# A four-layer graph network on one core: the turn of the count blocks one block later, the greatest key subtracted by PE, the normed rows added elsewhere

## The chip, the cores and the metric

The kernel runs on one core of a Trainium2 chip, in one launch. The metric is the device time in microseconds of that launch; lower is better. The engines are named PE (TensorE matmul), PEld (TensorE weight load), DVE (VectorE), ACT (ScalarE), POOL (GpSimd) and SP (SyncE, which here issues DMAs).

## The reference, cut to what matters

The input has 3125 nodes with 256 features and 100,000 edges, sorted by destination. Four layers follow each other; each adds a graph part and a mixer to x, and then a feed-forward part:

```python
xn = _layernorm(x, axis=-1)
x = x + _L0_gnn_ref(xn, edge_index, ...) + _L0_mix_ref(xn[None], ...)[0]
x = x + _L0_ffn_ref(_layernorm(x, axis=-1)[None], ...)[0]
...
```

Layer 0's graph part is a normalised sum over edges. It needs, for every pair of blocks of 125 nodes, how many edges lead from each source to each destination, and the number of edges into each destination (the degree). The mixers of layers 0 and 2 are linear attention:

```python
q = jax.nn.softmax(q, axis=-2) * SCALE
k = jax.nn.softmax(k, axis=-1)
context = jnp.einsum('bhdn,bhen->bhde', k, v)
out = jnp.einsum('bhde,bhdn->bhen', context, q)
...
return out + x
```

The softmax of the keys runs over all nodes. Layer 0's mixer gets the normed rows xn, and its result holds them once more (the "+ x" above). Layer 2's graph part gathers rows by source, weighs them and sums them by destination.

## The kernel before, in words

The nodes lie in 25 blocks of 125 rows: `self.x` and `self.xn` are 125 x 25 x 256 in SBUF, and `self.xt` is the transposed normed matrix. `PIECES` are groups of four blocks (the last has one).

The instructions are written through a layer that orders them for each engine when the kernel is built. So the order on an engine is not always the order of the text: an instruction can stand earlier or later among those that it does not depend on. `together` interleaves several generators by their progress, and `issue_after` puts instructions behind a given one on the same engine. Each engine then runs its own list strictly in order.

`prep` loads the edges, finds where each window of destinations begins and norms x. Then `l0_first` runs two generators beside each other.

- `counts` makes the count matrices. Two one-hot operands are built by DVE for every four runs of 128 edges (`lo`, L509, from the source's low part; `ky`, L512, from the source's block and the destination in its window). PE multiplies them into a bank `t` (L514; two banks), a group of windows at a time. ACT evacuates the group to `ct` (L517) and lets the accumulator sum the row (`chk`), which later tells whether a row has more than 255 edges. Each of the 25 destination blocks b has seven such groups, 175 in all. When a block's groups are done it is turned: PE transposes the 25 pieces of 125 x 125 in four portions of 8, 8, 8 and 1 through one bank `y` (L527), and `evac` copies each to `cd`, by turns on DVE (L179) and on ACT (L181). PE then sums columns (L532, into `dp`, from which the degrees come), SP stores `cd` to `cnt_d` (`move`, L172 and L173), DVE adds the identity to the diagonal of `ct` (L535), and every few blocks SP stores `ct` to `ctt_d`.
- `l0_mix_by_pieces` is layer 0's mixer. `context` first computes the greatest key of each column (L821 to L824), turns it into a row `kmrow`, and then for each block computes keys and values (`mm_tok`, L279), subtracts `kmrow` on DVE (L844), takes the exponential on ACT (L845), copies the values (L847) and adds to the context (L836, L837). After that the queries follow by pieces, and DVE adds the normed rows to x (L989) and the mixer's result (L990).

`l0_gnn` comes next: it scales the node rows (L616, L618, overwriting `self.xn`), reloads the counts from `cnt_d` (`cb`) and multiplies (L636). Layer 2's mixer calls the same `context` beside layer 2's graph part, in which POOL gathers rows (L2031), between about 2010 and 2540 us.

Of the kernel before, what the change touches and what calls it, by code (L numbers as in the profile page):

```python
# [2 lines left out]

# [9 lines left out]
F32 = mybir.dt.float32  # L13
# [110 lines left out]
class Net:  # L124
# [146 lines left out]
    def turn(self, src, dst):  # L271
        for i, w in PIECES:
            self.turn_piece(src, dst, i, w)

    def mm_tok(self, ps, xt, b, w):

        k = xt.shape[1]
        for h in range(k):
            self.nc.tensor.matmul(ps, xt[:, h, b * P:(b + 1) * P], w[:, h, :], start=(h == 0), stop=(h == k - 1))  # L279

# [156 lines left out]
    def counts(self, sb, rk, ck, wk, pt, px, py):  # L437
# [14 lines left out]
        nev = sum(-(-len(w) // (512 // (25 * r))) for r, w in WINDOWS)  # L452
        chk = sb.tile([P, nev], F32, name="chk")
# [35 lines left out]
        n = ev = 0  # L489
        full = None  # L490
        for b, (r, ws) in enumerate(WINDOWS):
# [9 lines left out]
            for w0 in range(0, nw, per):  # L501
                m = min(per, nw - w0)
                t = pt.tile([128, 512], F32, name="t")
                for w in range(m):
                    for j in range(ws[w0 + w][2]):
                        if n % 4 == 0:
                            wide = 25 * max(rs[n:n + 4])
                            lo = wk.tile([128, 128, 4], BF, name="lo", bufs=4)
                            nc.vector.tensor_tensor(lo, i4[:, :128], keys[:, 0, None, n:n + 4]  # L509
                                                    .to_broadcast([128, 128, 4]), op=OP.is_equal)  # L510
                            ky = wk.tile([128, 150, 4], BF, name="ky", bufs=4)
                            nc.vector.tensor_tensor(ky[:, :wide], i4[:, :wide], keys[:, 1, None, n:n + 4]  # L512
                                                    .to_broadcast([128, wide, 4]), op=OP.is_equal)
                        nc.tensor.matmul(t[:, w * 25 * r:(w + 1) * 25 * r], lo[:, :, n % 4],  # L514
                                         ky[:, :25 * r, n % 4], start=(j == 0), stop=(j == ws[w0 + w][2] - 1))
                        n += 1
                nc.scalar.activation(  # L517
                    ct[:, :, w0 * r:(w0 + m) * r].rearrange("p h (w r) -> p w h r", r=r),
                    t[:P, :m * 25 * r].rearrange("p (w h r) -> p w h r", w=m, r=r), AF.Identity,
                    accum_out=chk[:, ev:ev + 1])  # L520
                ev += 1
            cd = wk.tile([128, NB, P], BF, name="cd")
            for h0 in range(0, NB, 8):
                m = min(8, NB - h0)
                x = py.tile([128, 8, 128], BF, name="y")
                for h in range(m):
                    nc.tensor.transpose(x[:, h, :P], turned[:, h0 + h, :], self.ident_b[:P, :P])  # L527
                self.evac(cd[:, h0:h0 + m, :], x[:, :m, :P])
            cf = cd.rearrange("p h s -> p (h s)")
            for h in range(NB):  # L530
                m = 128 if h < NB - 1 else P
                nc.tensor.matmul(dp[:m, h:h + 1], cf[:, h * P:h * P + m], one, start=(b == 0 and h == 0),  # L532
                                 stop=(b == NB - 1 and h == NB - 1), skip_group_check=True)
            self.move(nc.sync, self.cnt_d[b], cf[3:])
            nc.vector.tensor_add(ct[:, b, :P], ct[:, b, :P], self.ident_b[:P, :P])  # L535
            if full is not None:
                self.move(nc.sync, *full)
                full = None
            if b + 1 in STORED:
                full = self.ctt_d[:, :, b0 * P:(b + 1) * P], ct4[:, :, 8:8 + (b + 1 - b0) * P]  # L540
            yield (b + 1) / NB
        self.move(nc.sync, *full)
        assert n == NE1 and ev == nev
# [4 lines left out]

        nc.vector.tensor_scalar(chk, chk, float(FEW), None, op0=OP.is_gt)
        nc.vector.tensor_reduce(self.viol[:P, 3:4], chk, axis=AX.X, op=OP.add)  # L550
# [42 lines left out]
    def l0_gnn(self):  # L593

        nc = self.nc
        with ExitStack() as s:
# [3 lines left out]
            w, bias = self.l0_w  # L600
            di = sb.tile([P, NB], F32, name="di")
# [211 lines left out]
    def context(self, sb, wk, w, wo, mem, share):  # L813
# [17 lines left out]
        nc.vector.tensor_copy(mrow, ps[:, :128])  # L831
# [8 lines left out]
        for b in range(NB):  # L840
            ps = self.bank()
            self.mm_tok(ps[:P, :256], self.xt, b, w[:, :, 128:384])
            k = wk.tile([P, 128], F32, name="k")
            nc.vector.tensor_sub(k, ps[:P, :128], mrow[:P])  # L844
            nc.scalar.activation(k, k, AF.Exp)  # L845
# [4 lines left out]
        if mem is not None:  # L850
            mk, mv, _ = mem
            nc.vector.tensor_sub(mk, mk, mrow[:mk.shape[0]])
            nc.scalar.activation(mk, mk, AF.Exp)
            add(mk, mv, False, True)
# [70 lines left out]
    def l0_mix_by_pieces(self, sb, wk):  # L925
# [19 lines left out]
        for i, c in PIECES:  # L945
# [17 lines left out]
            weighed = nc.vector.tensor_mul(q[:, :4 * n], q[:, :4 * n],  # L963
# [24 lines left out]
            with self.tc.issue_after(weighed.ins):  # L988
                nc.vector.tensor_add(v, v, self.xn[:, b0:b0 + n])  # L989
# [3 lines left out]
    def gen_l0_gnn(self):  # L993
        nc = self.nc
        with ExitStack() as s:
# [9 lines left out]
            y = sb.tile([P, NB, D], F32, name="y")  # L1005
            for b in range(NB):
# [1979 lines left out]
```

## Time and profile before

| what | before |
|---|---|
| median of 3 runs (lowest, highest) | 3721.22 us (3718.6, 3730.57) |
| profiled execution: time, span | 3728.88 us, 3727.0 us |
| mean granted clock of TensorE | 0.931 |
| busy: PE, PEld | 3317.4 us (89%), 2299.0 us (62%) |
| busy: DVE, ACT, POOL | 2403.4 us (64%), 1641.6 us (44%), 723.2 us (19%) |
| counting stage with layer 0's mixer | about 75 to 436 us of the span |
| layer 2's gathers | 2009.9 to 2537.0 us |

The page splits the span into 40 slices; the counting stage lies in the first five of them. Where a view gives a line such as L517, it is a line of the kernel before. A busy time is the union of an engine's instructions, so the durations of a group can sum to more than the busy time when they overlap. Each float32 matmul of this kernel shows as two passes, that is, as two records with two weight loads.

### The profile page before, as it was taken

To read this page: it belongs to the slowest core of one execution; us is meant where nothing else is said; L and a number is where in the kernel's file an instruction comes from. 1 tells how busy PE (TensorE), PEld (TensorE's weight loads), DVE (VectorE), ACT (ScalarE), POOL (GpSimd) and SP (SyncE) were. 2 spreads that over 40 slices of the span, in tenths; PEclk is the share of its full clock that TensorE was granted. 3 is DMA by queue.
4 is the path that set the end of the run, shared out by engine and by line. 5 is a ranking of instruction groups with operands and counts; after the bars stand their busy time and mean duration, and the time that the engine had idled before them with its cause. 6 is when DMAs were issued, how large, how long until landed. Compare 5 with 4: busy or idle time off the path is not lost. (4 is left out here: it accounts for less than half of the span.)

```text
span 3727.0 us, 61744 instructions
## 1 busy us (share of the span) xinstructions
PE 3317.4 (89%) x22027; PEld 2299.0 (62%) x22027; DVE 2403.4 (64%) x8119; ACT 1641.6 (44%) x3742; POOL 723.2 (19%) x702
## 2 busy tenths in 40 slices
PE   3887899699988979999998888998999999999978
PEld 2776699578866655555556677876663443444437
DVE  8878634875555673389246777886376666677663
ACT  3467500022235422223235566653337655556563
POOL 2000000144420420000003777771000000100011
PEclk9886799799989978999999999999999999999989
DMA  4234642356541110000004555445003222122135
GB/s 131 65 97 136 166 113 71 103 180 174 174 104 48 37 36 2 16 9 18 9 1 114 141 142 140 138 131 182 1 9 85 68 59 64 52 63 58 30 109 178
DMA packets 215258, 321.85 MB, mean 86 GB/s; under 512 B 51547, under 2 KB 159078, under 8 KB 214940
## 3 DMA queue, kind: packets, MB, share of 16 engines
q1 hardware_dynamic: 166346, 231.14, 21.7%
q0 software_dynamic: 40672, 83.85, 8.4%
q10 hardware_dynamic: 7922, 2.80, 0.3%
q8 instruction: 177, 2.90, 0.3%
q14 instruction: 141, 1.16, 0.1%
HBM read 248.17 MB, written 78.08 MB: 88 GB/s over the span
## 5 line engine op out<-in xcount | busy, mean ns | idle before, releaser
L2448 ACT ACTIVATE xn<-xn,us 125x1000 f32<-125x1000 f32 (+2 forms) x400 | 399.9, 1036 | 145.5 <-DVE z L2453 140.3
L2453 DVE SCALAR_TENSOR_TENSOR z<-xn,us,cs 125x1000 f32<-125x1000 f32 (+2 forms) x400 | 397.3, 1025 | 101.5 <-PE acc L2469 70.1
L2031 POOL DMA_INDIRECT hg<-hx_d,idx x405 | 402.3, 993 | 165.6 <-issue 101.8
L2469 PE MATMUL acc<-z,xr 125*32 125x500 f32 (+1 forms) x2800 | 367.6, 547 | 18.6 <-DVE z L2453 18.2
L1938 ACT ACTIVATE o<-ky,rest_d 128x50 bf16<-128x50 bf16 (+2 forms) x1190 | 303.1, 340 | 167.1 <-DVE ky L1929 147.4
L285 PE MATMUL ps<-xt,w 128*128 128x500 f32 (+1 forms) x672 | 277.7, 561 | 2.5 <-DMA w<-in_L_ffn_W_dram 1.5
L1661 DVE SCALAR_TENSOR_TENSOR x<-ps,lg,x 125x256 f32<-125x256 f32 x200 | 92.5, 478 | 245.3 <-PE ps L279 245.1
L2058 PE MATMUL acc<-hg,to 128*125 128x256 f32 x810 | 218.3, 410 | 12.3 <-DVE to L2054 11.5
L2469 PEld LDWEIGHTS acc<-z,xr 125*32 125x32 f32 x2800 | 100.1, 110 | 205.6 <-issue 116.1
L2469 PE MATMUL acc<-z,ones 125*32 125x500 f32 (+1 forms) x1400 | 223.8, 540 | 0.0
L636 PE MATMUL ps<-y,cb 125*125 125x256 bf16 x1875 | 209.1, 274 | 6.0 <-ACT y L623 2.7
L636 PEld LDWEIGHTS <-cb 125*125 125x125 bf16 x1875 | 206.2, 137 | 6.7 <-issue 5.9
L285 PEld LDWEIGHTS ps<-xt,w 128*128 128x128 f32 x672 | 125.3, 199 | 116.6 <-issue 103.3
L1650 ACT ACTIVATE h<-ps,bnb,bng 128x500 f32<-128x500 f32 (+1 forms) x112 | 80.5, 722 | 252.4 <-PE ps L285 252.4
L279 PE MATMUL ps<-wo,h 128*125 128x256 f32 x800 | 187.8, 386 | 3.5 <-ACT h L1655 2.6
L279 PEld LDWEIGHTS ps<-wo,h 128*125 128x125 f32 x800 | 142.8, 187 | 65.9 <-ACT h L1655 43.5
L285 PE MATMUL ps<-h,w 128*128 128x500 f32 (+1 forms) x448 | 179.3, 542 | 1.4 <-ACT h L1650 1.0
L2058 PEld LDWEIGHTS acc<-hg,to 128*125 128x125 f32 x810 | 151.8, 198 | 46.4 <-DVE to L2054 24.6
L514 PE MATMUL t<-ky,lo 128*128 128x75 bf16 (+4 forms) x1251 | 140.2, 253 | 34.8 <-ACT ct L517 19.7
L517 ACT ACTIVATE ct<-t 125x500 bf16<-125x500 f32 (+4 forms) x175 | 137.0, 831 | 76.3 <-PE t L514 73.9
L285 PE MATMUL pl<-xbt,w 128*128 128x256 f32 x560 | 152.7, 402 | 9.8 <-ACT xbt L1277 9.2
L2708 POOL DMA_DIRECT2D out_dram<-x x7 | 9.5, 1357 | 721.8 <-DVE x L2426 638.9
(696 smaller groups left out, 6910.4 us busy)
## 6 DMA issues: line engine op xcount, KB each, us to landing
w<-in_L_ffn_w_dram SPq DMA_DIRECT2D x70, 512.0 KB
cs<-ctt_d SPq DMA_DIRECT2D x100, 218.8 KB
lb<-low_d SPq DMA_DIRECT2D x76, 256.0 KB
w<-in_L_ffn_w_dram SPq DMA_DIRECT2D x18, 1024.0 KB
cnt_d<-cd SPq DMA_DIRECT2D x25, 683.6 KB
cb<-cnt_d SPq DMA_DIRECT2D x25, 683.6 KB
ctt_d<-ct SPq DMA_DIRECT2D x5, 2734.4 KB
cs<-ctt_d SPq DMA_DIRECT2D x50, 164.1 KB
```

The lines of the kernel that those rows point to most:

```text
L279: self.nc.tensor.matmul(ps, xt[:, h, b * P:(b + 1) * P], w[:, h, :], start=(h == 0), stop=(h == k - 1))
L285: self.nc.tensor.matmul(ps, w[:, h, :], xt[:, h, i:i + n], start=(h == 0), stop=(h == k - 1))
L514: nc.tensor.matmul(t[:, w * 25 * r:(w + 1) * 25 * r], lo[:, :, n % 4], ky[:, :25 * r, n % 4], start=(j == 0), stop=(j == ws[w0 + w][2] - 1))
L517: nc.scalar.activation(ct[:, :, w0 * r:(w0 + m) * r].rearrange("p h (w r) -> p w h r", r=r), t[:P, :m * 25 * r].rearrange("p (w h r) -> p ...
L636: nc.tensor.matmul(ps[:P, :D], cf[k][:, h * P:(h + 1) * P], y3[:, b0 + k, j, :], start=(k == 0 and j == 0), stop=(k == m - 1 and j == 2))
L1661: nc.vector.scalar_tensor_tensor(self.x[:, b, :], ps[:P, :D], g[:, b, e:e + 1], self.x[:, b, :], op0=OP.mult, op1=OP.add)
L1938: nc.scalar.activation(o1[:, k], ky[:, :, i], AF.Copy, scale=rest[:, k, n + i:n + i + 1])
L2031: nc.gpsimd.indirect_dma_start(out=hg[:, j, :], out_offset=None, in_=hx, in_offset=bass.IndirectOffsetOnAxis(ap=idx[:, c0 + j - CF:c0 + j ...
L2058: nc.tensor.matmul(acc, to, hg[:, j, :D], start=(c == first[kind]), stop=(c == last[kind]))
L2448: nc.scalar.activation(t[:, :n], (tail if one else rows)[:P, h, :n], AF.Relu, bias=us[:, 2, b, h:h + 1], scale=us[:, 0, b, h:h + 1])
L2453: made.append(nc.vector.scalar_tensor_tensor(zs[h], t[:, :n], us[:, 1, b, h:h + 1], c, op0=OP.add, op1=OP.mult).ins)
L2469: mm = nc.tensor.matmul(out[q:q + 32, :w], left, zs[h0 + j][:, k * w:k * w + w], start=(b == 0), stop=(b == NB - 1), tile_position=(0, q))
```

## The change

It has four parts. The evacuation of a window group no longer accumulates; whether there are too many edges is tested on the degrees instead (`many`). The turn of a block, its column sums, its stores and its diagonal are kept as functions in a list `late` and are called one by one behind the evacuations of the next block; all copies of a turned portion are on ACT. In `context` the row `kmrow` holds the negative maximum, and a matmul with one contracted row, written between the two halves of `mm_tok`, adds it to the keys in PSUM; the exponential reads PSUM. The addition of the normed rows leaves the mixer's pieces and is written at the start of `l0_gnn`.

```diff
-    def mm_tok(self, ps, xt, b, w):
+    def mm_tok(self, ps, xt, b, w, first=None):
         k = xt.shape[1]
         for h in range(k):
             self.nc.tensor.matmul(ps, xt[:, h, b * P:(b + 1) * P], w[:, h, :], start=(h == 0), stop=(h == k - 1))
+            if h == 0 and first is not None:
+                part, row = first
+                self.nc.tensor.matmul(part, self.ones[:1, :P], row[:1], start=False, stop=False, skip_group_check=True)
...
+        late = []
+        def turn(cd, turned, h0):
+            m = min(8, NB - h0)
+            x = py.tile([128, 8, 128], BF, name="y")
+            for h in range(m):
+                nc.tensor.transpose(x[:, h, :P], turned[:, h0 + h, :], self.ident_b[:P, :P])
+            nc.scalar.copy(cd[:, h0:h0 + m, :], x[:, :m, :P])
+        def close(b, cd, ct, done):
+            nonlocal full
+            cf = cd.rearrange("p h s -> p (h s)")
+            for h in range(NB):
...
+            self.move(nc.sync, self.cnt_d[b], cf[3:])
+            nc.vector.tensor_add(ct[:, b, :P], ct[:, b, :P], self.ident_b[:P, :P])
+            if full is not None:
+                self.move(nc.sync, *full)
+            full = done
...
                 nc.scalar.activation(
                     ct[:, :, w0 * r:(w0 + m) * r].rearrange("p h (w r) -> p w h r", r=r),
-                    t[:P, :m * 25 * r].rearrange("p (w h r) -> p w h r", w=m, r=r), AF.Identity,
-                    accum_out=chk[:, ev:ev + 1])
-                ev += 1
+                    t[:P, :m * 25 * r].rearrange("p (w h r) -> p w h r", w=m, r=r), AF.Identity)
+                if late:
+                    late.pop(0)()
+            while late:
+                late.pop(0)()
             cd = wk.tile([128, NB, P], BF, name="cd")
-            for h0 in range(0, NB, 8):
-                m = min(8, NB - h0)
-                x = py.tile([128, 8, 128], BF, name="y")
-                for h in range(m):
-                    nc.tensor.transpose(x[:, h, :P], turned[:, h0 + h, :], self.ident_b[:P, :P])
-                self.evac(cd[:, h0:h0 + m, :], x[:, :m, :P])
...
+            late += [partial(turn, cd, turned, h0) for h0 in range(0, NB, 8)]
+            done = (self.ctt_d[:, :, b0 * P:(b + 1) * P], ct4[:, :, 8:8 + (b + 1 - b0) * P]) if b + 1 in STORED else None
+            late.append(partial(close, b, cd, ct, done))
             yield (b + 1) / NB
+        for f in late:
+            f()
         self.move(nc.sync, *full)
...
-        nc.vector.tensor_scalar(chk, chk, float(FEW), None, op0=OP.is_gt)
-        nc.vector.tensor_reduce(self.viol[:P, 3:4], chk, axis=AX.X, op=OP.add)
+        many = sb.tile([P, NB], F32, name="many")
+        nc.vector.tensor_scalar(many, dp[:P, :NB], float(FEW), None, op0=OP.is_gt)
+        nc.vector.tensor_reduce(self.viol[:P, 3:4], many, axis=AX.X, op=OP.add)
...
@@ l0_gnn
+            for i, c in PIECES:
+                v = self.x[:, i // P:(i + c) // P]
+                nc.vector.tensor_add(v, v, self.xn[:, i // P:(i + c) // P])
...
@@ context
-        nc.vector.tensor_copy(mrow, ps[:, :128])
+        nc.vector.tensor_scalar(mrow, ps[:, :128], -1.0, None, op0=OP.mult)
...
-            self.mm_tok(ps[:P, :256], self.xt, b, w[:, :, 128:384])
+            self.mm_tok(ps[:P, :256], self.xt, b, w[:, :, 128:384], first=(ps[:P, :128], mrow))
             k = wk.tile([P, 128], F32, name="k")
-            nc.vector.tensor_sub(k, ps[:P, :128], mrow[:P])
-            nc.scalar.activation(k, k, AF.Exp)
+            nc.scalar.activation(k, ps[:P, :128], AF.Exp)
...
@@ l0_mix_by_pieces
-            with self.tc.issue_after(weighed.ins):
-                nc.vector.tensor_add(v, v, self.xn[:, b0:b0 + n])
             nc.vector.tensor_add(v, v, t[:, :n])
```

The general path, which does not run on this input, gets the same addition of the normed rows at its own graph part.

More of the change, by code (lines that the diff above doesn't have):

```diff
@@ L2 @@
 from contextlib import ExitStack
+from functools import partial
 import numpy as np
@@ L451, in counts @@
         keys = sb.tile([128, 2, NT1 * 128], BF, name="keys")
-        nev = sum(-(-len(w) // (512 // (25 * r))) for r, w in WINDOWS)
-        chk = sb.tile([P, nev], F32, name="chk")
         TB = 2
@@ L488, in counts @@
         dp = self.bank()
-        n = ev = 0
+        n = 0
         full = None
+        late = []
[9 more added lines that the diff above has]
+            for h in range(NB):
+                m = 128 if h < NB - 1 else P
+                nc.tensor.matmul(dp[:m, h:h + 1], cf[:, h * P:h * P + m], one, start=(b == 0 and h == 0),
+                                 stop=(b == NB - 1 and h == NB - 1), skip_group_check=True)
+            self.move(nc.sync, self.cnt_d[b], cf[3:])
[3 more added lines that the diff above has]
+            full = done
         for b, (r, ws) in enumerate(WINDOWS):
@@ L518, in counts @@
                     ct[:, :, w0 * r:(w0 + m) * r].rearrange("p h (w r) -> p w h r", r=r),
-                    t[:P, :m * 25 * r].rearrange("p (w h r) -> p w h r", w=m, r=r), AF.Identity,
-                    accum_out=chk[:, ev:ev + 1])
-                ev += 1
-            cd = wk.tile([128, NB, P], BF, name="cd")
-            for h0 in range(0, NB, 8):
-                m = min(8, NB - h0)
-                x = py.tile([128, 8, 128], BF, name="y")
-                for h in range(m):
-                    nc.tensor.transpose(x[:, h, :P], turned[:, h0 + h, :], self.ident_b[:P, :P])
-                self.evac(cd[:, h0:h0 + m, :], x[:, :m, :P])
[L529 to L540, printed above, removed]
+                    t[:P, :m * 25 * r].rearrange("p (w h r) -> p w h r", w=m, r=r), AF.Identity)
[3 more added lines that the diff above has]
+                late.pop(0)()
+            cd = wk.tile([128, NB, P], BF, name="cd")
+            late += [partial(turn, cd, turned, h0) for h0 in range(0, NB, 8)]
+            done = (self.ctt_d[:, :, b0 * P:(b + 1) * P], ct4[:, :, 8:8 + (b + 1 - b0) * P]) if b + 1 in STORED else None
+            late.append(partial(close, b, cd, ct, done))
             yield (b + 1) / NB
+        for f in late:
+            f()
         self.move(nc.sync, *full)
-        assert n == NE1 and ev == nev
+        assert n == NE1
         few = sb.tile([P, NB], F32, name="few")
@@ L851, in context @@
             mk, mv, _ = mem
-            nc.vector.tensor_sub(mk, mk, mrow[:mk.shape[0]])
+            nc.vector.tensor_add(mk, mk, mrow[:mk.shape[0]])
             nc.scalar.activation(mk, mk, AF.Exp)
@@ L962, in l0_mix_by_pieces @@
             nc.vector.reciprocal(qm[:, :4 * n], qm[:, :4 * n])
-            weighed = nc.vector.tensor_mul(q[:, :4 * n], q[:, :4 * n],
+            nc.vector.tensor_mul(q[:, :4 * n], q[:, :4 * n],
                                            qm[:, :4 * n, None].to_broadcast([P, 4 * n, 32]))
@@ L1005, in gen_l0_gnn @@
             y = sb.tile([P, NB, D], F32, name="y")
+            nc.vector.tensor_add(self.x, self.x, self.xn)
             for b in range(NB):
```

## The prediction

> **What bounds the kernel now.** I read the page first. PE is busy for 89% of the span, DVE for 64%, ACT for 44%, so the whole does not say which engine counts, and I went to the two places that the change touches. The first is the counting of edges beside layer 0's mixer (75 to 436 us of the span), the second layer 2's graph part (2010 to 2540 us). The busy times by stretch of the first, one line for each stretch (length, then PE, PEld, DVE, ACT, POOL busy, granted clock, DMA share, GB/s):
>
> ```profile
> 75.00:110.00 35.00, 24.71 (x254) 20.80 (x255) 33.89 (x130) 6.50 (x17) 0.00 (x0) 1.00 0.01 1
> 110.00:150.00 40.00, 36.41 (x310) 26.55 (x309) 33.32 (x107) 14.31 (x31) 0.00 (x0) 0.76 0.13 41
> 150.00:240.00 90.00, 80.67 (x816) 70.39 (x814) 62.48 (x205) 54.30 (x144) 0.21 (x1) 0.84 0.42 119
> 240.00:340.00 100.00, 81.60 (x865) 69.45 (x861) 83.21 (x237) 71.17 (x176) 0.43 (x2) 0.76 0.47 131
> 340.00:436.00 96.00, 75.85 (x697) 63.27 (x694) 73.76 (x191) 64.74 (x168) 0.42 (x2) 0.66 0.47 122
> ```
>
> Up to 110 us DVE is full (33.89 of 35). From 110 to 240 us PE is nearly full (117.1 of 130), DVE has 95.8 and ACT 68.6. From 240 to 436 us ("late" below) nobody is: PE 157.5, DVE 157.0, ACT 135.9 of 196 us, so there the engines wait for each other. Next I read what PE waited for in the late stretch (microseconds, times, longest):
>
> ```profile
> PE t L514 <- ACT ct L517: 14.2, 43, 0.6
> PE y L527 <- DVE cd L179: 8.5, 14, 1.2
> PE y L527 <- ACT cd L181: 7.5, 12, 1.1
> PE t L514 <- DVE ky L512: 2.0, 2, 1.7
> PE y L527 <- ACT ct L517: 1.8, 3, 0.8
> PE ps L532 <- ACT cd L181: 1.1, 5, 0.4
> ```
>
> PE turns a finished block of counts in four portions through one bank (y), and each portion waits until DVE or ACT has copied the one before: 8.5 + 7.5 + 1.1 = 17.1 us. From 110 to 240 us the same three rows have only 0.4 + 1.3 + 0.6 = 2.3 us, since there the mixer's matmuls fill the gaps. The durations I need, as groups of instructions from 75 to 440 us (busy us, mean ns of one | idle before):
>
> ```profile
> L517 ACT ACTIVATION_READ_ACCUMULATOR ct<-t 125x1 f32 x175 | 36.6, 209 | 0.0
> L179 DVE COPY cd<-y 128x1000 bf16<-128x1000 bf16 x50 | 34.0, 681 | 20.6 <-PE y L527 20.3
> L181 ACT COPY cd<-y 128x1000 bf16<-128x1000 bf16 x25 | 24.7, 989 | 36.4 <-PE y L527 36.2
> L836 PE MATMUL ps<-k,v 125*128 125x128 f32 x50 | 13.7, 365 | 0.0
> L989 DVE TENSOR_TENSOR x<-x,xn 125x1024 f32<-125x1024 f32 x6 | 7.3, 1218 | 0.0
> L844 DVE TENSOR_TENSOR k<-ps,kmrow 125x128 f32<-125x128 f32 x25 | 6.8, 287 | 16.7 <-PE ps L279 15.5 <-ACT cd L181 0.7 <-ACT ct L517 0.4
> L980 ACT ACT_TABLE_LOAD x6 | 7.7, 1283 | 0.1
> ```
>
> **Part 1: the turn of a block moves behind the next block's windows.** In the compiled order of the changed kernel the four turns and the column sums of block b stand between the seven window groups of block b+1, with window matmuls in between that need neither y nor cd. So a copy of 0.99 us has a group of PE work over it. I let the cd waits go: -17.1 late, -2.3 before that. The first turn of a block no longer waits for that block's last evacuation, the rows "y <- ct": 1.8 us late, 1.2 us from 110 to 240 us, so -3.0. What is late next is the evacuation ct, so it needs its own sum.
>
> **Part 2: ACT takes all copies, and the accumulators go.** DVE loses 50 copies, 34.0 us; ACT gains 50 x 0.989 = 49.5 us. ACT loses 175 accumulator reads. By the group that is 36.6 us, but the reads lie half over the evacuation they follow: at 427.60 us an evacuation of 0.77 us starts, its read runs from 428.19 to 428.38, and the next starts at 428.40, a step of 0.80. So a read costs between about 0.03 (0.80 - 0.77) and 0.21 us; I take 0.1, nearer to the step, 17.5 us in the stage. The compiled order has two more activation table loads in the mixer's pieces, 2 x 1.283 = 2.6 us. ACT gains 49.5 + 2.6 - 17.5 = 34.6 us in the stage and about 31.6 (32 copies of 16 blocks) + 2.6 - 11 (112 reads) = 23 us late, so 159 of 196 us: it becomes the fullest engine. In the late stretch ACT sat 31.1 us waiting for the transposes alone ("ACT cd <- PE y"), and these waits go with the new order, so the 23 us fit into time that is idle now. What stands behind a copy in ACT's queue is the next evacuation ct, for which PE waits with two banks. I set the copies ahead of evacuations against the shorter evacuations: 52 waits of PE for ct in the whole stage, some 0.1 us shorter each, -5, and +5 for the copies: 0. The ends are -5 (all hidden) and +45 (nearly every moved copy holds PE once); I stay near zero because ACT has 196 - 135.9 = 60 us free there. Half of the added table loads on the path: +1. The last block's turn has nothing after it: two copies on ACT instead of DVE, 2 x (0.989 - 0.681), +0.6. DVE's relief takes half of PE's waits for ky after 110 us (3.1 us), -1.5.
>
> One rule speaks against this part. The Trainium skill, page "ScalarE: Activation LUTs", section "Rules for kernel authors", sends plain element work to VectorE, which it calls up to about three times faster per element in bf16. The trace's copy out of PSUM has a ratio of 989 to 681 ns, 1.45. By the page's factor an estimate for the copy on DVE would be 0.33 us, the exchange would cost 50 x 0.66 = 33 us more ACT than DVE time instead of 50 x 0.31 = 15.4, and the last flush would lose 1.3 instead of 0.6 us.
>
> **Part 3: the greatest key by PE.** Per layer 25 subtractions leave DVE (25 x 0.287 = 7.2 us) and 25 matmuls with one contracted row come to PE, inside mm_tok between its two halves, with a weight load of their own. The nearest rows are float32 matmuls with 128 moving columns: 25 of them take 13.7 us in 50 passes (L836, with 4 contracted rows its passes are no shorter: 270 to 372 ns). From the start of one to the next matmul it was 0.28 us at full clock (210.65 to 210.93) and 0.53 us at half (224.09 to 224.62). At the stretch's clock of 0.84, a third of the time at half, that is 0.36 us: 25 x 0.36 = +9.0, between 7.0 and 13.7. It lies between 149 and 255 us, where PE is the fullest engine, so all of it is on the path. Below nothing is possible only through DVE: ACT's k waited 8.0 us for that subtraction, but PE waited for neither, so I give it no gain. In layer 2 the same 25 matmuls fall into a stretch that the gather queue sets. Two of its stretches by busy time, and then what POOL waited for from 2080 to 2400 us:
>
> ```profile
> 2150.00:2200.00 50.00, 41.28 (x411) 34.52 (x412) 36.65 (x161) 30.18 (x122) 38.12 (x40) 0.93 0.55 146
> 2200.00:2250.00 50.00, 47.35 (x522) 40.22 (x520) 42.12 (x163) 32.43 (x123) 38.42 (x39) 0.97 0.51 136
> ```
>
> ```profile
> POOL hg L2031 <- issue: 63.1, 207, 0.3
> ```
>
> POOL does 39 or 40 gathers in every 50 us with 0.30 us of issue between them, 1.25 us each, whatever PE does. PE has 3 to 9 us free in each 50 us, against 25 x 0.36 / 6 = 1.5 us that come in; this is the cover. Without it the layer would lose 9 us. I take +1 (0 to 9).
>
> **Part 4: the normed rows.** The seven additions (6 x 1.22 + 0.42 = 7.7 us of DVE) are written at the graph part's head, where 7.7 us would stand before the first scaling. But the compiled order has them in the counting stage, each directly or almost directly behind the addition of the mixer's piece: the same work a few instructions later, cost 0. Were they at the head, up to 7.7 us would be added. The queue of SP keeps its order except that one small store moves two places, and the last block's counts still go out before the reloads, so the 14 us between the last store's issue (436.5) and the first reload (450.8) stay.
>
> **Sum.** -17.1 - 2.3 - 3.0 + 0 + 1 + 0.6 - 1.5 + 9.0 + 1 + 0 = -12.3 us. The profiled execution took 3728.9 us (span 3727.0), 7.7 us above the median of 3721.2; 3728.9 - 12.3 = 3716.6 there, and 3709 us on the median.
>
> **The rivals.**
> Nothing is gained: the fullest engine stays 80% full, as now (157 of 196). With ACT at 159 the late stretch is 198 us, the cd waits come back as ct waits, while the early part has its 9.0 less 2.3 and 1.2: +7 us, 3728 us at the far end, about 3718 if half of the cd waits go. For it speaks that PE waits for ct oftener (43 times) than for cd (31), and that the compiled order leaves some late blocks with 23 to 27 window matmuls in one run and the turns in another; against it ACT's 31.1 us of waiting for turns.
> Slower: the copies in ACT's queue hold the evacuations, and PE stops with both banks t full. Each of the 50 moved copies that does so costs 0.99 us; 12.3 / 0.99 = 12 of them beyond my zero eat the gain, and with 25 it is +12 us, 3734; with all, +37 us, 3758. For it: ACT runs evacuations back to back at 425 to 430 us with PE waiting. It decides once ACT is over nine tenths full late.
> Much faster: the denser order keeps the clock up. If late PE ran at the 0.84 of 150 to 240 us, its 81.6 and 75.85 us would be 73.8 and 59.6, 24 us less: 3709 - 24 = 3685. Against it: the clock fell to 0.5 around 130 to 150 us with PE over eight tenths busy, so density alone does not hold it. The Trainium skill, page "TensorE: Matmul & The Clock Gate", Part 1, ties the low clock to an idle window of about 3.4 us. [...]
>
> **How the numbers follow.** Forecast (gain 5 to 20 us) 0.45, no gain 0.24, slower 0.19, much faster 0.12. 0.3% of the time, 11 us, is about what a measurement of this kernel can tell from no change. Three quarters of the forecast case and the fast one lie beyond it: faster 0.46; the rest of the forecast case and most of the no-gain case: same 0.33; slower 0.21. The range goes from the fast case, 3683, to the slower one with about 24 copies, 3733; the worst of the slow case and a little of the fast one lie outside.
>
> **What would show it.** Late: "PE y <- cd" nearly gone, ACT about 159 us busy and DVE about 135 (157 less 32 x 0.681); the counting ends some 12 us earlier than 436 us; gathers at 39 or 40 per 50 us. From 149 to 255 us 50 more PE passes of 0.27 us or more. Wrong if "PE t <- ACT ct" grows past 30 us, if ACT is nine tenths full, if the clock moves by 0.1, or if the time changes after the graph part's head.

## The result, and the profile after

The changed kernel takes 3735.7 us (median; 3730.8 to 3745.3), the kernel before 3728.2 us (median of as many runs beside it; 3718.6 to 3744.6). The ratio is 1.0019, 95% interval [1.0011, 1.0028]: about 7 us slower, where 12 us faster was forecast. (The forecast counted from 3721.2 us, the median of three runs of the kernel before; over twenty runs that median is 3728.2, so 7 of the 27 us between the forecast 3709 and 3735.7 us lie in the starting point.) The profiled execution took 3737.6 us (span 3735.7), against 3728.9 (span 3727.0).

The stretches of the counting part again, with the columns of the table of before:

```profile
75.00:110.00 35.00, 25.36 (x233) 19.99 (x234) 33.05 (x127) 5.04 (x9) 0.00 (x0) 1.00 0.00 1
110.00:150.00 40.00, 36.34 (x352) 28.06 (x351) 34.10 (x114) 23.21 (x28) 0.00 (x0) 0.83 0.13 41
150.00:240.00 90.00, 87.65 (x911) 74.53 (x910) 53.69 (x181) 65.79 (x119) 0.21 (x1) 0.92 0.43 120
240.00:340.00 100.00, 81.23 (x869) 72.48 (x869) 80.06 (x232) 86.91 (x145) 0.42 (x2) 0.76 0.48 132
340.00:436.00 96.00, 65.17 (x608) 53.63 (x606) 51.49 (x135) 69.37 (x114) 0.42 (x2) 0.64 0.47 121
```

Up to 240 us the change does what it should: PE is busier (149.4 us in 75 to 240 us against 141.8), the granted clock is higher (0.92 for 0.84 in the third row), and the mixer's first product (here and below: of the queries with the context) comes at 259.6 instead of 271.1 us. The late stretch gives it back: PE 146.4 of 196 us where it had 157.5, DVE 131.6 where it had 157.0, ACT 156.3. The last one-hot operand is built at 420.7 instead of 427.0 us, but the last block's store goes out at 437.2 instead of 436.0. What PE waited for from 240 to 436 us (microseconds, times, longest):

```profile
PE t L538 <- ACT ct L541: 18.8, 35, 3.2
PE y L499 <- ACT cd L500: 18.6, 23, 3.4
PE ps L507 <- ACT cd L500: 3.6, 7, 1.1
PE t L538 <- DVE ky L536: 3.2, 3, 2.6
PE y L499 <- ACT ct L541: 2.6, 6, 1.0
```

The waits of the turns for their copies ("y <- cd", "ps <- cd") were 17.1 us. They are 22.2 us now, all of them for ACT, and the longest is 3.4 us instead of 1.2. What lies in such a wait is seen in ACT's own timeline (start, duration, operation; in brackets the idle time before it):

```profile
391.73 0.74 ACT L541 ACTIVATE ct<-t 125x500 bf16<-125x500 f32 x1
392.50 1.28 ACT L995 ACT_TABLE_LOAD   x1
393.79 0.20 ACT L995 ACTIVATE ss<-ss 125x4 f32<-125x4 f32 x1
394.01 1.28 ACT L974 ACT_TABLE_LOAD   x1
395.31 0.31 ACT L974 ACTIVATE q<-q 125x128 f32<-125x128 f32 x1
395.52 0.97 ACT L500 COPY cd<-y 128x1000 bf16<-128x1000 bf16 x1
397.58 0.99 ACT L500 COPY cd<-y 128x1000 bf16<-128x1000 bf16 x1 [1.09 <-PE y L499]
```

and in PE's, where one line answers to it:

```profile
396.55 1.00 PE L499 MATMUL y<-ident_b,ct 125*128 125x125 bf16 x8 [3.39 <-ACT cd L500]
```

The turn ahead of it was done at 391.7 us, but its copy stands in ACT's list behind an evacuation and the mixer's square root and exponential with a table load each. Until 396.5 us nobody may write bank y, and PE stops with everything behind that turn. Then a portion takes 2.07 us each: PE writes y (1.0 us), ACT copies it (0.99), and each idles while the other works (1.09).

Not all waits are of this kind. In 18 of the 30 behind the 22.2 us, 11.9 us together, ACT began the copy within 0.1 us of the turn's end, and PE had less other work than the copy takes before the next turn or column sum. So it is at the stage's end (a line of ACT, then one of PE):

```profile
433.10 0.99 ACT L500 COPY cd<-y 128x1000 bf16<-128x1000 bf16 x1 [1.09 <-PE y L499]
434.14 1.00 PE L499 MATMUL y<-ident_b,ct 125*128 125x125 bf16 x8 [0.92 <-ACT cd L500]
```

In the other 12 waits, 10.3 us, ACT began the copy 0.5 to 10 us after the turn's end.

The groups the prediction spoke of, from 75 to 440 us:

```profile
L541 ACT ACTIVATE ct<-t 125x500 bf16<-125x500 f32 x96 | 78.7, 860 | 27.2 <-PE t L538 25.5 <-PE y L499 1.0
L500 ACT COPY cd<-y 128x1000 bf16<-128x1000 bf16 x75 | 75.4, 1006 | 40.8 <-PE y L499 38.4 <-issue 1.2 <-PE t L538 0.7
L283 PE MATMUL ps<-kmrow,ones 1*125 1x128 f32 x50 | 12.6, 333 | 0.0
L616 DVE TENSOR_TENSOR x<-x,xn 125x1024 f32<-125x1024 f32 x6 | 7.3, 1210 | 0.0
```

ACT still waits 38.4 us for turns in the whole stage for these 75 copies (36.2 us before for 25 of them; DVE had 20.3 for the other 50). From 240 to 436 us it is 29.8 us (24.7 for the long copies, 5.1 for the short), where the prediction took 31.1 us of such waits as idle time that would become free.

The second place is layer 2. From the first gather to the last sum over gathered rows it took 541.4 us before and 548.9 us after, and layer 2's gathering began at nearly the same moment (2009.9 and 2010.6 us), since some 3 us by which layer 0 was behind (the first reload of the counts came at 453.9 instead of 450.8 us) were made up on the way. POOL's gathers (shortest, median and longest in ns, then first and last start):

```profile
L2045 POOL DMA_INDIRECT hg<-hx_d,idx x405: 942/949/2162, 2010.6 to 2543.0; - x135
```

Before, the last started at 2537.0 us.

### The profile page after: what moved, and what is told of

Its sections match the earlier page's. It is cut to its first block, busy times and chain, and to the rows that moved or that the text cites. A ratio compares the mean times of both kernels' runs of the same rounds, so it can differ in the third digit from the quotient of the medians.

```text
span 3735.7 us, 61750 instructions
## 1 busy us (share of the span) xinstructions
PE 3321.8 (89%) x22127; PEld 2302.7 (62%) x22127; DVE 2364.4 (63%) x8019; ACT 1681.6 (45%) x3619; POOL 725.2 (19%) x702
## 3 DMA queue, kind: packets, MB, share of 16 engines
q1 hardware_dynamic: 166346, 231.14, 22.2%
## 5 line engine op out<-in xcount | busy, mean ns | idle before, releaser
L2483 PE MATMUL acc<-z,xr 125*32 125x500 f32 (+1 forms) x2800 | 367.1, 548 | 19.2 <-DVE z L2467 18.8
L533 DVE TENSOR_TENSOR lo<-i,keys 128x512 bf16<-128x512 bf16 x313 | 131.1, 419 | 62.7 <-PE t L538 61.7
L538 PE MATMUL t<-ky,lo 128*128 128x75 bf16 (+4 forms) x1251 | 137.1, 254 | 34.7 <-ACT ct L541 20.2
L541 ACT ACTIVATE ct<-t 125x500 bf16<-125x500 f32 (+3 forms) x175 | 137.1, 836 | 37.4 <-PE t L538 35.5
```

Source lines behind the costliest of these rows:

```text
L541: nc.scalar.activation(ct[:, :, w0 * r:(w0 + m) * r].rearrange("p h (w r) -> p w h r", r=r), t[:P, :m * 25 * r].rearrange("p (w h r) -> p ...
L2483: mm = nc.tensor.matmul(out[q:q + 32, :w], left, zs[h0 + j][:, k * w:k * w + w], start=(b == 0), stop=(b == NB - 1), tile_position=(0, q))
```

## The experiments

The runs were made on several chips. On those of e5 to e8 and e13 to e18 the kernel before takes 3951 to 3960 us instead of some 3728, so ratios are to the kernel before on the same chip, and moments of the counting part are compared with e16, the changed kernel itself there. On that kind of chip the changed kernel itself has one run, e16: 3971.2 us where the kernel before has 3959.9, 1.0028. "Counting ends" is the issue of the last store of a block's counts. Moments and stretches are read from one profiled execution of each kernel.

**The parts alone (e1 to e3).** e1 has only the counting part of the change; e2 only the key by PE; e3 is the changed kernel with layer 2's key subtracted by DVE again:

```diff
+            if mem is None:                       # layer 2
+                self.mm_tok(ps[:P, :256], self.xt, b, w[:, :, 128:384])
+                nc.vector.tensor_add(k, ps[:P, :128], mrow[:P])
+                nc.scalar.activation(k, k, AF.Exp)
...
```

> Only the counting part of the change (turns one block later, all copies on ACT, no accumulators); the greatest key and the normed rows as before. Theory A (in the counting stage DVE stops at the diagonal addition and so gives the gain back; the 7.6 us lost after 2005 us belong to the key matmuls in layer 2): the counting stage ends near 436 us, layer 2 costs nothing, the time is that of before within 4 us. Rival B (the key matmuls in the counting stage ate a gain of the turns): the counting stage ends near 427 us and the time is about 9 to 12 us below before.

> Only the greatest key by PE, in both layers; the rest as before. Theory A: layer 2 loses about 7 us, the counting stage 0 to 5 us: 7 to 12 us above before. Rival C (the loss in layer 2 is a matter of the order that the counting part brings, or noise of one profile): 0 to 2 us above before, or 9 us in the counting stage and nothing in layer 2.

> The changed kernel, but in layer 2 DVE adds the negative greatest key and no key matmul is run there. Theory A: layer 2's last product of gathered rows ends some 7 us earlier than in the changed kernel for the same start of the gathers, and the time is 7 us below the changed kernel, near that of before. Rival C: no difference from the changed kernel within 3 us.

Ratios 1.0001 [0.9992, 1.0010], 0.9996 [0.9988, 1.0005] and 1.0010 [1.0001, 1.0020]. Counting ended at 433.4, 431.5 and 440.7 us. Neither part alone is slower than before; both together are. The price of the key in layer 0 depends on what stands beside it: without deferral the mixer's first product comes earlier with it (271.1 to 265.4 us), with deferral later (252.6 to 259.6). Layer 2's stretch is 545.3, 545.2 and 541.9 us. So e3's stretch is the 7 us shorter that was expected, but its median is only 3.4 us below the changed kernel's, with intervals that overlap.

**The diagonal, the copying engine, the normed rows (e4 to e6).** e4 adds the identity to a block's diagonal one block later, e5 gives half of the copies back to DVE, e6 puts the normed rows back into the mixer's pieces.

```diff
-            nc.vector.tensor_add(ct[:, b, :P], ct[:, b, :P], self.ident_b[:P, :P])
+            while diag:                                   # e4, in close
+                c = diag.pop(0)
+                nc.vector.tensor_add(c, c, self.ident_b[:P, :P])
+            diag.append(ct[:, b, :P])
...
-            nc.scalar.copy(cd[:, h0:h0 + m, :], x[:, :m, :P])
+            self.evac(cd[:, h0:h0 + m, :], x[:, :m, :P])  # e5, in turn
...
+            with self.tc.issue_after(weighed.ins):        # e6, in the mixer's pieces
+                nc.vector.tensor_add(v, v, self.xn[:, b0:b0 + n])
```

> The changed kernel, with the diagonal addition of block b put behind the turns of block b+1 instead of its own. Theory A: DVE no longer waits for the turns there (20.8 us from 340 to 437 us and 5.8 us from 240 to 340 us), window matmuls follow sooner, and the counting stage ends about 10 us earlier, at some 427 us; the time is about 3726. Rival D (ACT, with all copies, binds the late stretch): the waits of DVE move to the one-hot builders and the stage ends within 3 us of 437.

> The changed kernel with the copies of turned portions by turns on DVE and ACT, as before. Theory F (the turns that are left behind the last one-hot operands, 15.7 us in the changed kernel against 8.3 before, take back what the counting won): the chain of that tail has three copies of 0.99 us of which one or two become 0.68, so 1 to 3 us below the changed kernel. Rival D (ACT, which has all copies, binds the late stretch): 8 us or more below it.

> The changed kernel with the normed rows added in the mixer's pieces, as before. The prediction's term (0, since the compiled order had the additions in the counting stage anyway): within 3 us of the changed kernel. Rival E (the new place costs something in the counting stage): 4 to 8 us below the changed kernel.

Ratios 1.0023 [1.0012, 1.0035], 1.0053 [1.0035, 1.0071] and 1.0050 [1.0032, 1.0068]; counting ended at 445.5, 438.6 and 440.4 us (e16: 439.2). None of the three is the cause. That ACT takes all copies is not what costs: with DVE back in, the waits of turns and sums for copies from 240 to 430 us are still 16.2 us (20.2 in the changed kernel). The Trainium skill, page "ScalarE: Activation LUTs", section "Rules for kernel authors", sends plain element work to VectorE; here half of the copies on VectorE moved the end by 0.6 us, less than two profiles of one kernel differ (437.2 and 439.2 us).

**A second bank (e7), and the key in layer 0 alone (e8).** e7 is the changed kernel with the turned portions alternating between bank y and the bank x of the window keys; e8 is the kernel before with the key by PE in layer 0 only.

```diff
-            x = py.tile([128, 8, 128], BF, name="y")
+            x = (px.tile([128, 8, 128], BF, name="x") if h0 // 8 % 2 else py.tile([128, 8, 128], BF, name="y"))
```

> The changed kernel with two PSUM banks by turns for the turned portions (the second is the bank that the keys used at the start), so that PE can turn a portion while ACT copies the one before. Theory F: the tail behind the last one-hot operands falls from 15.7 to about 10 us and the waits of PE for a copy (15.5 us from 340 to 437 us) go: 5 to 10 us below the changed kernel. Rival D: ACT's copies keep the pace, 0 to 2 us below.

> The kernel before with the greatest key by PE in layer 0 only. From the profiles (the key part alone ended the counting 4.5 us earlier and lengthened layer 2 by about 4.6 us): layer 2 as before, the counting some 4 us shorter, so about 4 us below before, at 3725. Rival: the shorter counting was noise of one profile, and the time is that of before.

Ratios 1.0037 [1.0019, 1.0055] and 1.0001 [0.9981, 1.0020]. With two banks counting ended at 430.3 us, 9 us before e16. PE's waits for copies from 240 to 436 us in e7:

```profile
PE ps L507 <- ACT cd L500: 8.7, 15, 1.5
PE y L499 <- ACT cd L500: 6.1, 8, 1.9
PE x L499 <- ACT cd L500: 0.8, 2, 0.5
```

The portions wait 6.9 us instead of 17.7 (e16), but the column sums 8.7 instead of 3.6, so 15.6 us in all instead of 21.3. e8's counting ended at 430.4 us, as its expectation had it, but the whole doesn't show the 4 us: its interval holds both that gain and none.

**Twice the key, the last blocks in place, and two candidates (e9 to e12).** e9 runs the one-row matmul twice with half of the maximum. e10 turns the last two blocks behind their own window groups. e11 is the changed kernel with two banks and with layer 2's key on DVE; e12 is the kernel before with two banks and layer 0's key by PE, so without deferral.

```diff
-                self.nc.tensor.matmul(part, self.ones[:1, :P], row[:1], start=False, stop=False, skip_group_check=True)
+                for _ in range(2):                # e9, and mrow times -0.5
+                    self.nc.tensor.matmul(part, self.ones[:1, :P], row[:1], start=False, stop=False, skip_group_check=True)
...
             late.append(partial(close, b, cd, ct, done))
+            while late and b >= NB - 2:           # e10
+                late.pop(0)()
```

> The changed kernel with the one-row matmul done twice for each block, each with half of the greatest key, so 50 instead of 25 of them in each of the two layers. Theory (the one-row matmuls are paid on PE, in layer 0 where PE is full and in layer 2 too, where the forecast gave them only 1 us): layer 0's stage ends 3 to 9 us later and the stretch from the first gather to the last sum of layer 2 grows by another 4 to 5 us, some 8 to 13 us over the changed kernel, ratio to before about 1.004 to 1.006. Rival (the loss in layer 2 is one of order, not of PE time): layer 2's stretch stays at about 547 us and the whole within 4 us of the changed kernel, ratio about 1.002.

> The changed kernel, but the last two of the 25 blocks are turned behind their own window groups instead of one block later, so that nothing but one block's turn is left behind the last one-hot operand. Theory (the loss of the counting part is the tail of turns that nothing fills): the time from the last ky to the last store falls from 16.5 us to 9 to 11 us, and the counting stage ends at about 430 to 432 us instead of 437; the whole gains 5 to 7 us over the changed kernel, ratio to before about 1.000. Rival (the tail only shows work that was late already): the last ky comes as much later as the tail gets shorter, the end stays at 436 to 438 and the ratio at 1.002.

> The changed kernel with two banks for the turned portions and with the greatest key subtracted by DVE again in layer 2. Theory (the two places that lose are the chain through one bank at the end and the one-row matmuls of layer 2): counting ends 6 to 9 us earlier than in the changed kernel, layer 2's stretch is 4 to 5 us shorter, 10 to 13 us in all, so 3 to 6 us below before, ratio 0.9985 to 0.999. Rival (the two do not add up, since the clock takes back what the order gives): the same as before or slower, ratio 1.000 to 1.001.

> The kernel before with the key subtracted by PE in layer 0 alone, and with two banks for the turned portions, whose copies DVE and ACT share as before; neither the deferred turns nor the change of the normed rows. Theory (the waits of turns for copies, 17 us late, can be had by a second bank, without deferring anything): counting ends 3 to 8 us before 436 us and the whole is 3 to 8 us below before, ratio 0.998 to 0.999. Rival (the bank taken from the window keys and the clock give it back): no difference, ratio 1.000.

e9: 1.0065 [1.0051, 1.0080]. Counting ended 19 us later than in the changed kernel (456.4), 0.77 us for each of 25 more matmuls, twice what the prediction took. Of this only 0.42 us are PE's own time, from the first pass of such a matmul to the start of the next one (mean of 50). Layer 2's stretch was 548.0 us, no longer than with one (548.9): there the rival was right.
e10: 1.0020 [1.0010, 1.0031]. The time from the last one-hot to the last store fell from 16.5 to 10.3 us, but the last one-hot came 6.5 us later (427.2), and counting ended at 437.5. I had taken the long tail for the cause; it is not. The rival held: it only shows work that is late already.
e11: 0.9990 [0.9981, 0.9999], counting ended at 427.9. e12: 0.9981 [0.9970, 0.9992], counting ended at 422.4, median 3720.0 against 3727.6 us. The version without deferral has the lower median of the two, by 3.5 us, though the intervals overlap.

**Is it the order? (e13 to e16).** In the changed kernel's compiled order the turns of late blocks stand in pairs or threes with 20 to 30 window matmuls in one run before them, not one by one as the text has them. e13 pins PE to the text, e14 does so with e11's edits, e15 is the kernel before with the second bank and nothing else, e16 the changed kernel again.

```diff
+            with self.tc.issue_after(put[0].ins):         # in turn: behind the last window matmul
                 for h in range(m):
-                    nc.tensor.transpose(x[:, h, :P], turned[:, h0 + h, :], self.ident_b[:P, :P])
+                    put[0] = nc.tensor.transpose(x[:, h, :P], turned[:, h0 + h, :], self.ident_b[:P, :P])
...
+                        with self.tc.issue_after(put[0].ins) if put[0] is not None else ExitStack():
                             mm = nc.tensor.matmul(t[:, w * 25 * r:(w + 1) * 25 * r], lo[:, :, n % 4],
```

> The changed kernel with its PE order pinned to the text: every turned portion issues behind its window group and ahead of the next one, so that 4 to 10 window matmuls stand between two portions all through the stage. Theory (the deferral brought nothing because the compiled order puts the turns together again): the waits of the turns for copies after 240 us fall from 19.5 us to below 8, the counting stage ends at 425 to 431 us instead of 437, the whole 6 to 12 us below the changed kernel, ratio to before 0.999 to 1.001. Rival (one bank and ACT's queue of evacuations and mixer work set the pace in any order): the waits move to the window matmuls (t for ct above 25 us after 240 us), the stage ends at 435 us or later, ratio 1.001 to 1.004.

> As e13, but with two banks for the turned portions and with the greatest key subtracted by DVE in layer 2. Theory: what is left of the waits goes, counting ends at 420 to 427 us, and the whole is 5 to 12 us below before, ratio 0.997 to 0.9985. Rival (ACT's queue is the bound): no better than the two banks without the pinned order, 428 us and ratio 0.999.

> The kernel before with two banks for the turned portions and nothing else changed. Theory (the 17 us of waits of turns for copies belong to the single bank): these waits fall to about 6 us after 240 us, counting ends 4 to 9 us earlier than 436 us, ratio 0.998 to 0.999. Rival (the gain of the earlier run with two banks came from the key by PE in layer 0): the waits fall but the stage ends within 3 us of 436, ratio 1.000.

> The changed kernel once more, for a second profile. Theory: the same waits in the late stretch (turns for copies 19 to 20 us, windows for evacuations 18 to 19), the counting ending between 435 and 440 us, and layer 2's stretch from first gather to last sum between 546 and 550 us. If these move by more than 4 us, differences of that size between single profiles say nothing.

e13: 1.0041 [1.0021, 1.0061], counting ended at 438.4. PE's waits from 240 to 436 us in e13:

```profile
PE y L501 <- ACT cd L502: 32.7, 16, 5.3
PE ps L509 <- ACT cd L502: 6.7, 9, 1.3
PE t L541 <- ACT ct L545: 6.7, 18, 0.5
PE y L501 <- ACT ct L545: 4.9, 12, 1.0
```

So the compiled order alone was not at fault: the stage ends where the rival put it, though not by the rival's waits. The window groups now wait less for evacuations (6.7 us), but fewer and longer waits stand at the turns; 29.3 of the 39.4 us are behind a copy that ACT began more than 0.2 us after the turn's end. At 342.1 us PE was done with the windows behind a turn and then stood 5.08 us before the next turn, while ACT worked through evacuations, two table loads and the mixer's activations ahead of the copy (lines of ACT, then one of PE):

```profile
342.24 0.60 ACT L545 ACTIVATE ct<-t 125x500 bf16<-125x500 f32 x1
342.86 1.28 ACT L999 ACT_TABLE_LOAD   x1
344.15 0.20 ACT L999 ACTIVATE ss<-ss 125x4 f32<-125x4 f32 x1
344.37 1.28 ACT L978 ACT_TABLE_LOAD   x1
345.67 0.63 ACT L978 ACTIVATE q<-q 125x512 f32<-125x512 f32 x1
346.20 0.97 ACT L502 COPY cd<-y 128x1000 bf16<-128x1000 bf16 x1
347.23 1.00 PE L501 MATMUL y<-ident_b,ct 125*128 125x125 bf16 x8 [5.08 <-ACT cd L502]
```

e15: 0.9979 [0.9962, 0.9997], counting ended at 424.2 us. The same view of e15:

```profile
PE t L514 <- ACT ct L517: 16.4, 49, 0.7
PE t L514 <- DVE ky L512: 7.2, 8, 2.8
PE x L527 <- ACT cd L181: 2.2, 2, 1.1
PE ps L532 <- DVE cd L179: 1.9, 5, 0.4
PE y L527 <- ACT ct L517: 1.7, 3, 0.7
...
PE y L527 <- DVE cd L179: 1.3, 2, 1.0
```

The waits for copies are 5.9 us in all by PE's list (0.5 us of it in a row not shown), and they did not come back as waits for evacuations (16.4 for 14.2); only the waits for the one-hot ky rose, by 5 us. One bank more does what the deferral was to do. Not all of the 12 us reach the graph part: the first reload of the counts came 20 us after the last store (at 444.5 us, in e12 at 442.6), in the other kernels 15 to 17, so it is 6 us earlier than before (450.8). e14: 0.9979 [0.9961, 0.9997], counting ended at 430.2, no earlier than in e11, and with 21.1 us of waits for copies, as many as in e16. So the end of the stage doesn't go by these waits alone. e16: waits of 17.7, 3.6 and 19.3 us in the first three kinds, counting ended at 439.2, so single profiles of one kernel agree within some 2 us here. Layer 2's stretch was 783.1 us on that chip, so its expected moment holds only for the others.

**The two that were left (e17, e18).** All kernels with deferred turns have the mixer's last product at 395 to 420 us and then 23 us or more of counting alone; those without have it 1 to 13 us ahead of the end. e17 reports the counting's progress a block later, so that the mixer is written a block later. e18 keeps both PE's matmul and DVE's addition in layer 2, half of the maximum each.

```diff
-            yield (b + 1) / NB
+            yield b / NB                          # e17
...
-            nc.scalar.activation(k, ps[:P, :128], AF.Exp)
+            if mem is None:                       # e18; mrow times -0.5 in layer 2
+                nc.vector.tensor_add(k, ps[:P, :128], mrow[:P])
+                nc.scalar.activation(k, k, AF.Exp)
```

> The changed kernel, but the counting reports its progress one block later, so that the mixer's work is interleaved one block later. Theory (the late stretch loses since the deferral brings the mixer's end ahead and leaves counting alone): the mixer's last product moves from 401 us to 415 us or later, the counting ends at 427 to 433 us instead of 437, the whole 4 to 10 us below the changed kernel, ratio to before 0.999 to 1.001. Rival (the one bank holds the counting whatever lies beside it): the mixer ends later, the counting still at 436 us or later, ratio 1.001 to 1.003.

> The changed kernel, but in layer 2 PE adds half of the negative maximum and DVE the other half, so that the one-row matmul and DVE's addition are both there. Theory (what costs in layer 2 is PE's matmul between the halves): the stretch from the first gather to the last sum stays at 546 to 550 us, or at 4 us above that of a kernel without the matmul on the same chip, ratio as the changed kernel's, 1.002. Rival (what costs is the other order that the missing addition brings): the stretch goes back to 541 to 545 us, ratio 1.000 to 1.001.

e17: 1.0052 [1.0031, 1.0073]. The mixer's last product moved to 411.0 us and the late waits of y for cd fell to 13.5 us, but those of the column sums rose to 10.4, and counting ended at 443.8: the clock from 150 to 240 us was 0.72 where the changed kernel has 0.92, and the lead was gone by 240 us. The stage went as the rival had it, and the whole is above its range, as in other kernels on these chips (e5, e6). Since the clock fell as well, the run doesn't show whether the empty end costs anything. e18: 1.0065 [1.0043, 1.0088], layer 2's stretch 793.5 us, the longest of all. Giving DVE its addition back does not help, so what is left is the matmul or the order that it brings.

**Layer 2 over all runs**, from the first gather to the last sum, in us:

| | chips with before at 3728 us | chips with before at 3951 to 3960 us |
|---|---|---|
| key by DVE in layer 2 | before 541.4, e1 545.3, e3 541.9, e11 544.9, e12 545.0; mean 543.7 | e8 756.9, e14 770.0, e15 773.6; mean 766.8 |
| key by PE in layer 2 | after 548.9, e2 545.2, e4 548.6, e10 547.9; mean 547.7 | e5 783.4, e6 776.0, e7 779.8, e13 782.6, e16 783.1, e17 784.2; mean 781.5 |
| key by PE, twice / PE and DVE | e9 548.0 | e18 793.5 |

In the mean the kernels with the matmul take 4 us longer on the first kind of chip and 15 us on the second. These are single profiles: on the first kind the two rows meet at 545.2 and 545.3 us, and e8's profile is of a run 12 us below its median (without it the 15 are 10 us).

## Why the prediction was wrong

**The step that failed first: "So a copy of 0.99 us has a group of PE work over it. I let the cd waits go: -17.1 late."** They did not go: 22.2 us late. Half of them (11.9 us) stand behind a copy that began at once: there the compiled order has too little PE work over it, the turns in pairs or threes. For the other half (10.3 us) the prediction asked what stands between two turns on PE, and not what stands before the copy on ACT. With one bank, a turn can only start once the copy of the one before is *done*, and that copy sits in ACT's list behind evacuations and the mixer's activations (3.39 and 5.08 us in the lines above). Work put between two turns helps only as far as that. e13 had the order that the step assumed and waited more; e7 and e15 had a second bank and waited less. The diagnosis was right in the main (e15 is without 11 of the 17 us, its graph part begins to reload 6 us earlier and the whole is 8 us faster, with an interval of 1 to 15), the remedy was not. The -2.3 early did not come either: from 110 to 240 us the waits for copies are 2.4 us (1.8 + 0.6), moved to before 150 us. The early part of "y <- ct" did (0.2 us left of 1.2); its late part rose from 1.8 to 2.6 us.

**Part 2 by its sizes was right, by its verdict not.** ACT was put at 159 us late and has 156.3; DVE at 135 and has 131.6. Waits for ct rose from 14.2 to 18.8 us, far below the 30 that would have made the rival. The -1.5 for the one-hot ky did not come (waits of 3.8 us after 110 us, 3.1 before). What was missed is that an engine four fifths full can still hold another by its order.

**The last flush, +0.6, was mis-sized:** from the last one-hot to the last store it is 16.5 us instead of 9.0. But e10 shows that shortening it gains nothing, so it is not where the 7 us are.

**The key in layer 0, +9.0: not a fixed price.** Its passes take 12.6 us, near the row of 13.7 us that they were sized by. Added to the kernel before it filled PE's idle time (PE busy from 110 to 240 us: 117.1, with it 125.7 of 130; granted clock 0.82, with it 0.86) and the stage ended some 4 us earlier; the prediction had called all of it on the path, and had dismissed DVE's 8.0 us that ACT waited for. Added to the deferred turns it moved the mixer's first product back by 7.0 us, the low end of its range; a second one cost 19 us. PE was hardly fuller there than in the kernel before (118.6 of 130 us in e1, 124.0 with the key), but the clock went the other way (0.91, with the key 0.89). Why the price differs is open.

**The key in layer 2, +1 (0 to 9): mis-sized.** The cover was said to be PE's 3 to 9 us idle in each 50 us. The profiles show some 4 us for the first and nothing for a second one, so it is not PE time by the count. On the chips where gathers are slower the difference is 10 to 15 us. There POOL waits for PE most of the time that it is idle: from 2040 to 2700 us 218.5 us in e15 (acc, t and ps together) and 217.6 in e16, where on the first kind of chip the same three waits are 19.1 us before and 18.8 after. That the gathers' pace holds "whatever PE does" was wrong there, and on the first kind too strong: the view that it was read from also has waits for PE, of 6.7 us for acc and 3.4 for t, which the prediction did not count. What inside the stretch makes the difference stays open. PE's compiled order in it changes with the matmul: on the first kind of chip PE waits from 2010 to 2560 us 21 to 28 us for DVE's `turned` and 11 to 14 for its `to` in the five kernels without it, 8 to 11 and 28 to 32 in the four with it. No run has the matmul without this order, and e18 rules out only the missing addition.

**The normed rows, 0:** right (e6: counting ended at 440.4 us, in e16 at 439.2). The 14 us between the last store and the first reload, which were to stay, became 16 (437.7 to 453.9). **The clock:** the rival with a denser order got its clock up to 240 us (0.89 for 0.82 from 110 to 240 us) and not after (0.70 for 0.71). From 401 to 437 us the changed kernel is granted 0.59, and no wait of PE listed there is over 1.1 us; the idle window of some 3.4 us in the Trainium skill, page "TensorE: Matmul & The Clock Gate", Part 1, doesn't account for that. The same part also tells of a kernel whose clock swings by frequent short idle times of PE between groups of matmuls; no run here shows that: from 150 to 240 us the clock was 0.72 in e17 with PE busy for 84.8 of 90 us, and 0.84 before with 80.7.

The rival "nothing is gained" came nearest: the waits stay in another form, and its far end was +7 us on the stage. Taken over the whole, some 4 us of the loss are layer 2's (the medians of after and e3, and the table above; in this pair of profiles 7.5 of 8.7 us) and the rest is the counting part's, where the stage's end, 4 us earlier by the key alone, comes 1 to 3 us later with the deferral (after and e16). Why key and deferral do worse together than either alone was not settled.

## What to carry to other kernels

When a producer waits for its bank, ask where the copy that frees the bank stands in the copying engine's list: work put between two producers doesn't help if the copy is late, and a second bank does. Compare what the deferral of a step and what a second buffer would do before writing the deferral. A matmul that replaces an addition on another engine has no price of its own: it ended one stage 4 us earlier, set another back by 7 us, and went with a longer time in a stretch that PE did not seem to bound.

## What the runs showed of the hardware

The same program takes 3728 us on some chips and 3951 to 3960 on others. Most of it lies in layer 2's gathers: from 2040 to 2540 us POOL does 73 to 79 of them per 100 us on the first (before and after) and 54 to 63 on the second (e15 and e16), though the median gather is as long (949 ns in after and in e16); there POOL waits, mostly for PE. PE in turn is busy for only 68 to 82 us of each 100 there, and most of its waits have no releaser in the view ("issue"), so what sets the pace on these chips is not shown. The granted clock differed by a quarter between kernels in the same stretch, on two chips: 0.72 with PE busy 84.8 of 90 us (e17), 0.98 with 89.7 (e12), both from 150 to 240 us. A float32 matmul with one contracted row is no cheaper than one with 125: its passes take 333 ns in the mean, the others 330 (both with 128 columns, in the counting stage of the changed kernel).
